# A mixture-of-experts layer on one core: all batches routed, results returned by accumulating DMA

## The chip, the cores and the metric

The kernel runs on one core of a Trainium2 chip. A core has five engines with a queue each: PE (TensorE, matrix products into PSUM), DVE (VectorE), ACT (ScalarE), POOL (GpSimd) and SP (SyncE, which here only starts DMA transfers). Each queue runs in order, and engines wait for one another by semaphores. Sixteen DMA engines move data between the chip's memory (HBM) and the on-chip memory (SBUF). The metric is the time of one execution in microseconds (us).

## The reference, cut to what matters

Sixteen sequences of 512 tokens with 256 numbers each go through a causal attention layer and a feed-forward layer, both behind a layernorm and with a residual:

```python
x = x + attention(layernorm(x))            # 16 heads of 64, soft-clamped scores
t = layernorm(x).reshape(-1, 256)          # 8192 tokens
shared = gelu(t @ sw1 + sb1) @ sw2 + sb2   # every token
probs = softmax(t @ gate_w + gate_b)       # 8 experts
topk_p, topk_i = top_k(probs, 2)           # two experts of each token
h = gelu(einsum('td,edf->etf', t, w1) + b1)
y = einsum('etf,efd->etd', h, w2) + b2
x = x + shared + sum over the two chosen experts of topk_p * y
```

All matrices of an expert are 256x256, and everything is float32.

## The kernel before, in words

**Attention.** The 16 batches run one after the other, and each as 8 pairs of heads. The loop at L826 steps over the 128 pairs. A step issues the scores of the next pair, attends the present one (`attend`), projects queries and keys of the pair after next (`project_qk`), and calls `around(b, p, fill)`, which places the rest of the work at fixed steps p of a batch. The order of PE is the program's own (L817); the other engines' queues are ordered by the compiler's scheduler, and the transfers of SP are held to the program's order (`sync_dma`).

**Feed-forward of the batch before.** Beside the attention of batch b, `around` does batch b - 1: its output projection (p = 0, 1), layernorm (p = 1), transposes, shared hidden layer and gate (p = 3), and at p = 4 `place` (where each token's two rows go), the shared output (`expert_out` with e = 8, where a product of `comb` and `b2_sb` at L722 adds all biases weighted by the gate) and `scatter` (eight indirect DMAs on POOL).

**Routing.** Batches 0 to 8 and 9 to 14 form two groups (L20). `scatter` writes each normalised token into two rows of `xs`, one region per expert. When a group is complete, `tabulate` works out which expert each tile of 256 rows belongs to (L84 gives the number of tiles: 43 and 31), and `routed_steps` puts one step per tile into a queue of fillers: load rows and weights two steps ahead (`fetch`, `fetch_weights`), hidden layer (`routed_hidden`), transposes of the next tile (`turned`), output of the tile before (`routed_out`), stored to `ys`. The queue is popped by `fill`, which spreads it over the remaining steps of attention.

**Gathers.** After the tiles come `pack` and `gather_steps`: for each 128 tokens two indirect DMAs fetch the rows of `ys` (L653), DVE scales and adds them to the residual, which had been kept in HBM (L668), and SP stores the result.

**Batch 15** is not routed. After the attention its feed-forward runs at L841 to L856, with the second group's fillers between: all eight experts on all 512 tokens (`hidden`, `expert_out`, L848 to L854), and the gathers of the second group beside them.

Of the kernel before, what the change touches and what calls it, by code (L numbers as in the profile page):

```python
# [19 lines left out]
GROUPS = (9, 6)  # L20
# [4 lines left out]
def preln_attention_moe_kernel(  # L25
# [23 lines left out]
    SH = E  # L49
    FC = w1.shape[3] // P  # L50
# [26 lines left out]
    class Group:  # L77


        def __init__(self, g, first, count):  # L80
            self.g, self.first, self.count = g, first, count
            self.tokens = count * N
            self.stride = self.tokens + SLOTS
            self.tiles = (2 * self.tokens + E * (SLOTS - 1)) // SLOTS  # L84
            self.rows = E * self.stride + E * SLOTS
            self.xs = dram.tile([self.rows, D], F32, tag=f"xs{g}", name=f"xs{g}")
            self.ys = dram.tile([self.tiles * SLOTS, D], F32, tag=f"ys{g}", name=f"ys{g}")
            self.kept = dram.tile([count, N, D], F32, tag=f"kept{g}", name=f"kept{g}")
            self.writes, self.stores = [], []
            self.slots, self.shares, self.places = {}, {}, None  # L90
            self.running = None
# [30 lines left out]
    b2_sb = weights("b2_sb", b2, nc.sync)  # L122
# [32 lines left out]
    zeros = const.tile([P, D], F32, tag="zeros", name="zeros")  # L155
    nc.gpsimd.memset(zeros, 0.0)

    def counting(name, n, step):
        i = const.tile([P, n], I32, tag=f"{name}_i", name=f"{name}_i")
        nc.gpsimd.iota(i, pattern=[[step, n]], base=0, channel_multiplier=0)  # L160
# [6 lines left out]
    by_slot = counting("by_slot", n_most, SLOTS)  # L167
    region = {}
    for group in dict.fromkeys(group_of.values()):
        region[group] = counting(f"region{group.g}", E, group.stride)  # L170
        for i in range(E):
# [4 lines left out]
                    zeros.unsqueeze(1).to_broadcast([P, SLOTS // P, D]),  # L176
                ).ins
            )
        group.places = const.tile(
            [P, group.count, NT, 2], F32, tag=f"places{group.g}", name=f"places{group.g}"  # L180
        )
# [4 lines left out]
    def layernorm(src, name):  # L186
# [10 lines left out]
        xn = work.tile([P, NT, D], F32, tag="xn", name=f"xn_{name}")  # L197
        for t in range(NT):
            nc.vector.tensor_scalar(  # L199
                xn[:, t, :],  # L200
# [161 lines left out]
    def gate(b, xT):  # L362

        pg = ps_m.tile([P, NT, E], F32, tag="m", name=f"pg_{b}")
        for t in range(NT):
# [29 lines left out]
        comb = small.tile([P, NT, 32], F32, tag="comb", name=f"comb_{b}")  # L395
        nc.gpsimd.memset(comb, 0.0)
        nc.gpsimd.memset(comb[:, :, E : E + 1], 1.0)
        nc.vector.scalar_tensor_tensor(
            comb[:, :, :E], rank, 1.5, pr, ALU.is_lt, ALU.mult
        )  # L400
        return comb, rank, pr

    def place(b, rank, pr):

        group = group_of[b]
        chosen = small.tile([P, NT, E], F32, tag="chosen", name=f"chosen_{b}")
# [10 lines left out]
        nc.vector.tensor_add(slot, pos, region[group].unsqueeze(1).to_broadcast([P, NT, E]))  # L417
        slots = const.tile([P, NT, 2], I32, tag=f"slots{b}", name=f"slots_{b}")
        shares = const.tile([P, NT, 2], F32, tag=f"shares{b}", name=f"shares_{b}")
        for i in range(2):  # L420
            own = small.tile([P, NT, 2, E], F32, tag="own", name=f"own_{b}_{i}")
            nc.vector.scalar_tensor_tensor(
                own[:, :, 0, :], rank, float(i), slot, ALU.is_equal, ALU.mult
            )
            nc.vector.scalar_tensor_tensor(
                own[:, :, 1, :], rank, float(i), pr, ALU.is_equal, ALU.mult
            )
            both = small.tile([P, NT, 2], F32, tag="both", name=f"both_{b}_{i}")
            nc.vector.tensor_reduce(both, own, AX.X, ALU.add)
            nc.vector.tensor_copy(group.places[:, b - group.first, :, i], both[:, :, 0])  # L430
            nc.vector.tensor_copy(shares[:, :, i], both[:, :, 1])
        nc.vector.tensor_copy(slots, group.places[:, b - group.first])
        group.slots[b], group.shares[b] = slots, shares
# [22 lines left out]
    def tabulate(group):  # L456
# [34 lines left out]
        which = small.tile([P, K], F32, tag="which", name=f"which_{g}", bufs=1)  # L491
# [23 lines left out]
        group.skip = skip  # L515
        for e in range(E):
            with queued():
# [3 lines left out]
                    zeros.unsqueeze(1).to_broadcast([P, SLOTS // P, D]),  # L521
            )
            unordered(f"xs{g}", inst, group.writes)

    def pack(group):

        g = group.g
        places = group.places.rearrange("p b t i -> p (b t i)")
        n_places = group.count * NT * 2
        over = small.tile([P, n_places, E - 1], F32, tag="table", name=f"over_{g}", bufs=2)  # L530
        nc.vector.tensor_tensor(
            over,
            places.unsqueeze(2).to_broadcast([P, n_places, E - 1]),
            region[group][:, 1:].unsqueeze(1).to_broadcast([P, n_places, E - 1]),
            ALU.is_ge,
        )
        nc.vector.tensor_mul(
            over, over, group.skip[:, : E - 1].unsqueeze(1).to_broadcast([P, n_places, E - 1])
        )
        back = small.tile([P, n_places], F32, tag="back", name=f"back_{g}", bufs=1)  # L540
        nc.vector.tensor_reduce(back, over, AX.X, ALU.add)
        nc.vector.tensor_sub(back, places, back)
        packed = const.tile([P, group.count, NT, 2], I32, tag=f"packed{g}", name=f"packed_{g}")
# [199 lines left out]
    def fill(p):  # L743

        if not fillers:
            return
# [162 lines left out]
```

## Time and profile before

| | |
|---|---|
| median of 3 runs | 2317.4 us (2316.65 to 2320.81) |
| the profiled execution | 2317.56 us, of which the span of its instructions is 2315.8 us |
| granted clock of PE | 0.993 of full speed |
| busy | PE 95%, DVE 48%, ACT 45%, POOL 41% of the span |
| batches 0 to 8 routed, first group's table | at 1151 us |
| second group's table | at 2061 us |
| last attention step's matmuls end | about 2096 us |
| output projection of batch 15 starts | 2104.4 us |
| dense experts of batch 15 start | 2238.4 us |
| moved by DMA | 161 MB |

The profile is of one execution. In its timelines a line gives start, duration, engine, line of the kernel, operation, and output<-input, and in square brackets how long the engine had stood idle and who released it. PE's instructions overlap, so the durations printed add up to more than the time; the difference between two starts is what an instruction costs. A float32 product counts as two instructions.

### The profile page before, as it was taken

To read this page: it belongs to the slowest core of one execution; us is meant where nothing else is said; L and a number is where in the kernel's file an instruction comes from. 1 tells how busy PE (TensorE), PEld (TensorE's weight loads), DVE (VectorE), ACT (ScalarE), POOL (GpSimd) and SP (SyncE) were. 2 spreads that over 40 slices of the span, in tenths; PEclk is the share of its full clock that TensorE was granted. 3 is DMA by queue.
4 is the path that set the end of the run, shared out by engine and by line. 5 is a ranking of instruction groups with operands and counts; after the bars stand their busy time and mean duration, and the time that the engine had idled before them with its cause. 6 is when DMAs were issued, how large, how long until landed. Compare 5 with 4: busy or idle time off the path is not lost.

```text
span 2315.8 us, 29554 instructions
## 1 busy us (share of the span) xinstructions
PE 2209.4 (95%) x10968; PEld 1405.6 (61%) x10968; DVE 1102.8 (48%) x1858; ACT 1037.9 (45%) x1352; POOL 952.3 (41%) x1091
## 2 busy tenths in 40 slices
PE   7999999999999999999999999999999799899996
PEld 3555555556565555555667677667655465558874
DVE  3445454545363636363644434444446555453334
ACT  3544444444444545444444554554554444351211
POOL 3444443435353535344423412422455847450025
PEclk9999999999999999999999999999999999999999
DMA  5001010101010101010142342342230503035776
GB/s 191 1 1 37 1 37 1 37 1 37 1 37 1 37 1 37 1 37 1 37 147 59 118 128 64 101 128 82 84 97 20 153 7 119 21 100 168 224 228 208
DMA packets 119855, 161.34 MB, mean 70 GB/s; under 512 B 12320, under 2 KB 90144, under 8 KB 119200
## 3 DMA queue, kind: packets, MB, share of 16 engines
q1 hardware_dynamic: 107760, 125.62, 17.5%
q0 software_dynamic: 11520, 31.47, 4.4%
q10 hardware_dynamic: 432, 2.36, 0.3%
q8 instruction: 87, 1.43, 0.3%
q14 instruction: 56, 0.46, 0.1%
HBM read 99.64 MB, written 59.77 MB: 69 GB/s over the span
## 4 chain that ended last, share of the span: by engine, by line
PE 76%; DVE 11%; DMA 5%; issue 3%; ACT 3%; POOL 2%; SPq 0%; POOLq 0%; DVEq 0%; ACTq 0%
PE pq L249 15%; PE s L272 10%; PE av L323 10%; PE po L353 9%; PE pv L232 8%; PE ry L604 5%; PE rh L586 5%; DVE oT L342 4%; PE sums L332 4%; DMA part<-ys,packed 3%; PE ph L695 2%; PE py L714 2%; DVE xn_a L199 2%; PE pr L573 1%; PE py L722 1%
## 5 line engine op out<-in xcount | busy, mean ns | idle before, releaser
L287 ACT ACTIVATE pe<-s 128x768 f32<-128x768 f32 (+1 forms) x384 | 334.5, 874 | 704.8 <-PE s L272 679.1
L342 DVE RECIPROCAL oT<-sums 128x256 f32<-128x256 f32 x256 | 430.9, 1724 | 355.3 <-PE sums L332 355.2
L291 POOL TENSOR_SCALAR_AFFINE_SELECT pe<-pe 128x256 f32<-128x256 f32 (+1 forms) x384 | 192.0, 501 | 902.0 <-ACT pe L288 847.4
L272 PE MATMUL s<-qk 64*128 64x512 f32 (+3 forms) x2048 | 345.4, 456 | 11.9 <-ACT qk L256 11.5
L288 ACT ACTIVATE pe<-pe 128x768 f32<-128x768 f32 (+1 forms) x384 | 349.5, 914 | 10.9
L323 PE MATMUL av<-pe,v 128*64 128x512 f32 (+3 forms) x2048 | 307.8, 443 | 34.5 <-DVE oT L343 34.4
L272 PEld LDWEIGHTS s<-qk 64*128 64x128 f32 x2048 | 176.6, 186 | 200.7 <-issue 144.9
L323 PEld LDWEIGHTS av<-pe,v 128*64 128x64 f32 x2048 | 140.3, 138 | 241.7 <-issue 208.7
L249 PE MATMUL pq<-xT_a,wq_sb 128*128 128x512 f32 x512 | 252.8, 617 | 0.8 <-DVE xT_a L217 0.8
L249 PE MATMUL pq<-xT_a,wk_sb 128*128 128x512 f32 x512 | 241.6, 595 | 5.0 <-DVE x L360 3.5
L232 PE MATMUL pv<-wv_sb,xT_a 128*128 128x256 f32 x1024 | 233.6, 382 | 4.4 <-DVE xT_a L217 4.4
L303 POOL TENSOR_TENSOR added<-pe,pe 128x768 f32<-128x768 f32 x128 | 232.3, 1814 | 10.5
L256 ACT COPY qk<-pq 128x512 f32<-128x512 f32 x256 | 149.8, 585 | 178.0 <-PE pq L249 178.0
L232 PEld LDWEIGHTS pv<-wv_sb,xT_a 128*128 128x128 f32 x1024 | 195.1, 192 | 52.0 <-issue 24.4
L353 PE MATMUL po<-wo_sb,oT 128*128 128x256 f32 x1024 | 226.3, 380 | 0.0
L353 PEld LDWEIGHTS po<-wo_sb,oT 128*128 128x128 f32 x1024 | 195.2, 191 | 38.7 <-issue 14.3
L653 POOL DMA_INDIRECT part<-ys,packed x120 | 117.2, 977 | 154.4 <-DMA dw<-in_w 99.6
L249 PEld LDWEIGHTS pq<-xT_a,wk_sb 128*128 128x128 f32 x512 | 97.7, 191 | 129.1 <-issue 120.4
L595 ACT ACTIVATE rhT<-rh,biases 128x256 f32<-128x256 f32 x148 | 62.0, 470 | 253.5 <-PE rh L586 253.4
L307 POOL TENSOR_TENSOR added<-added,pe 128x512 f32<-128x512 f32 x128 | 163.5, 1277 | 10.7
L239 DVE COPY v<-pv 128x512 f32<-128x512 f32 x128 | 87.3, 689 | 144.9 <-PE pv L232 144.9
L586 PE MATMUL rh<-rT,ew 128*128 128x256 f32 x592 | 142.6, 385 | 6.3 <-DVE rT L577 5.5
(134 smaller groups left out, 2302.4 us busy)
## 6 DMA issues: line engine op xcount, KB each, us to landing
ew<-in_w SPq DMA_DIRECT2D x148, 256.0 KB, 3.1
rows<-xs SPq DMA_DIRECT2D x74, 256.0 KB, 3.1
ys<-y SPq DMA_DIRECT2D x74, 256.0 KB, 3.3
x<-in_x SPq DMA_DIRECT2D x16, 512.0 KB, 4.0
xs<-zeros SPq DMA_DIRECT2D x32, 256.0 KB, 4.3
kept<-x SPq DMA_DIRECT2D x15, 512.0 KB, 3.0
acc<-kept SPq DMA_DIRECT2D x60, 128.0 KB, 2.9
out<-acc SPq DMA_DIRECT2D x60, 128.0 KB, 2.4
```

The lines of the kernel that those rows point to most:

```text
L232: nc.tensor.matmul(pv[:, u], xT[:, k, t * P : (t + 1) * P], wv_pairs[:, k, :, 2 * g : 2 * g + 2, :], start=(k == 0), stop=(k == KD - 1),)
L249: nc.tensor.matmul(pq, w[:, k, p * P : (p + 1) * P], xT[:, k, :], start=(k == 0), stop=(k == KD - 1),)
L272: nc.tensor.matmul(ps[:, i, at : at + w], qk[rows, 1, j * P : (j + 1) * P], qk[rows, 0, j * P :], start=True, stop=True,)
L287: nc.scalar.activation(pe[:, :, :w], ps[:, :, :w], AF.Tanh, scale=CLAMP_IN)
L288: nc.scalar.activation(pe[:, :, :w], pe[:, :, :w], AF.Exp, scale=SOFTCLAMP)
L291: nc.gpsimd.affine_select(out=diagonal, in_=diagonal, compare_op=ALU.is_ge, fill=0.0, base=0, pattern=[[0, 2], [0, n], [1, P]], channel_mu ...
L303: nc.gpsimd.tensor_tensor(added, pair_pe[b, p, 0][:, :, P:], pe[:, :, : N - P], ALU.add)
L307: nc.gpsimd.tensor_tensor(added[:, :, P:], added[:, :, P:], pe[:, :, : 2 * P], ALU.add)
L323: nc.tensor.matmul(po[i * DH : (i + 1) * DH, j * P :], v[:, j, i, p % 2, :], pair_pe[b, p, u][:, i, at : at + w], start=(j == 0), stop=(j ...
L342: nc.vector.reciprocal(oT[:, half], sums[:, half])
L353: nc.tensor.matmul(po[:, u, :], oTs[b, c][:, t * P : (t + 1) * P], wo_sb[:, c, :], start=(c == 0), stop=(c == NP - 1),)
L586: nc.tensor.matmul(ph[:, f, :], tile["w1"][:, d, f * P : (f + 1) * P], tile["T"][:, d, :], start=(d == 0), stop=(d == KD - 1),)
```

## The change

All 16 batches are routed, in groups of 12 and 4 (55 and 23 tiles by the same formula), so batch 15's dense pass goes. `xs` rows grow from 256 to 272 numbers: the tail holds the token's number and, for each of its two choices, slot, expert and gate value, which `place` writes behind the normalised token. The residual with the shared output is stored straight to `out` by SP. Each tile's result gets its expert's output bias by DVE (a fourth load per tile, spread over the partitions), is scaled on ACT by the token's share, and is added to the rows of `out` by two indirect DMAs of 128 rows each that accumulate in memory. Rows that hold no token carry a number past the bound and are left out. The pair of DMAs of a tile waits for the pair of the tile before, and the first pair of a group for the stores of its batches. `pack`, `gather_steps`, `comb` with its transpose, and the bias product on PE are gone; the shared output bias is added to the residual by POOL. Loads run three steps ahead. Sixteen steps of the first group are kept for the end.

The diff, cut to its core:

```diff
-GROUPS = (9, 6)
+GROUPS = (12, 4)
+META = 16
...
-            self.xs = dram.tile([self.rows, D], F32, tag=f"xs{g}", name=f"xs{g}")
-            self.ys = dram.tile([self.tiles * SLOTS, D], F32, tag=f"ys{g}", name=f"ys{g}")
-            self.kept = dram.tile([count, N, D], F32, tag=f"kept{g}", name=f"kept{g}")
+            self.xs = dram.tile([self.rows, ROW], F32, tag=f"xs{g}", name=f"xs{g}")
...
-    b2_sb = weights("b2_sb", b2, nc.sync)
+    sb2 = const.tile([P, D], F32, tag="sb2", name="sb2")
+    nc.sync.dma_start(sb2, b2[SH : SH + 1, 0].to_broadcast([P, D]))
...
     def place(b, rank, pr, xn2):
+        nc.gpsimd.memset(xn2[:, :, D:], 0.0)
...
+        nc.vector.tensor_scalar(xn2[:, :, TOK], by_token, float((b - B) * N), None, ALU.add)
         for i in range(2):
+            own = small.tile([P, NT, 3, E], F32, tag="own", name=f"own_{b}_{i}")
+            for j, of in enumerate((slot, expert, pr)):
+                nc.vector.scalar_tensor_tensor(
+                    own[:, :, j, :], rank, float(i), of, ALU.is_equal, ALU.mult
+                )
+            at = CHOICE + 3 * i
+            nc.vector.tensor_reduce(xn2[:, :, at : at + 3], own, AX.X, ALU.add)
+            nc.vector.tensor_copy(slots[:, :, i], xn2[:, :, at])
...
     def fetch_weights(group, tile):
+        tile["b2"] = work.tile([P, D], F32, tag="eb2", name=f"eb2_{g}_{k}", bufs=4)
+        sync_dma(tile["b2"], b2[bass.ds(e, 1), 0].to_broadcast([P, D]))
...
     def routed_out(group, tile):
-        y = work.tile([P, SUB, D], F32, tag="y", name=f"y_{g}_{k}", bufs=2)
-        nc.vector.tensor_copy(y, py)
-        inst = sync_dma(
-            group.ys[k * SLOTS : (k + 1) * SLOTS].rearrange("(u p) d -> p u d", p=P), y
+        y = work.tile([P, SUB, D], F32, tag="y", name=f"y_{g}_{k}", bufs=3)
+        nc.vector.tensor_add(y, py, tile["b2"].unsqueeze(1).to_broadcast([P, SUB, D]))
+        choices = tile["rows"][:, :, CHOICE : CHOICE + 6].rearrange("p u (i c) -> p u i c", c=3)
+        part = small.tile([P, SUB, 2], F32, tag="part", name=f"part_{g}_{k}", bufs=3)
+        nc.vector.scalar_tensor_tensor(
+            part, choices[:, :, :, 1], group.which[:, k : k + 1], choices[:, :, :, 2],
+            ALU.is_equal, ALU.mult,
         )
-        group.stores.append(inst)
+        share = small.tile([P, SUB], F32, tag="share", name=f"share_{g}_{k}", bufs=3)
+        nc.vector.tensor_reduce(share, part, AX.X, ALU.add)
+        tile["token"] = small.tile([P, SUB], I32, tag="token", name=f"token_{g}_{k}", bufs=3)
+        nc.vector.tensor_scalar(tile["token"], tile["rows"][:, :, TOK], float(B * N), None, ALU.add)
+        for u in range(SUB):
+            nc.scalar.activation(y[:, u], y[:, u], AF.Copy, scale=share[:, u : u + 1])
+        tile["y"] = y
+
+    def returned(group, tile):
+        insts = []
+        for u in range(SUB):
+            inst = nc.gpsimd.indirect_dma_start(
+                out=out.rearrange("b n d -> (b n) d"),
+                out_offset=bass.IndirectOffsetOnAxis(ap=tile["token"][:, u : u + 1], axis=0),
+                in_=tile["y"][:, u],
+                in_offset=None,
+                bounds_check=B * N - 1,
+                oob_is_err=False,
+                compute_op=ALU.add,
+            ).ins
+            to_results(inst, group.added or group.stores)
+            insts.append(inst)
+        group.added = insts
+
+    def to_results(inst, made):
+        tc.add_to_no_dep_group("results", inst)
+        behind(inst, made)
+        tc.declare_no_dep(inst, group="results", keep=made, reason="other tokens, or behind those kept")
...
         def step(k):
+            begin(k + 3)
             if k < 0:
-                begin(k + 2)
                 return
-            begin(k + 2)
...
-            if k >= 1:
-                routed_out(group, live.pop(k - 1))
+            if 1 <= k <= group.tiles:
+                routed_out(group, live[k - 1])
+            if k >= 2:
+                returned(group, live.pop(k - 2))
+        return [lambda k=k: step(k) for k in range(-3, group.tiles + 2)]
...
+    AT_END = 16
     def fill(p):
-        if not fillers:
+        if len(fillers) <= AT_END:
             return
-        pace["due"] += len(fillers) * WEIGHT[p] / max(pace["left"], WEIGHT[p])
+        pace["due"] += (len(fillers) - AT_END) * WEIGHT[p] / max(pace["left"], WEIGHT[p])
...
-            xns[done, 1] = layernorm(x_tiles[done], f"f{done}")
+            xns[done, 1] = layernorm(x_tiles[done], f"f{done}", ROW)
+            nc.gpsimd.tensor_tensor(
+                x_tiles[done],
+                x_tiles[done],
+                sb2.unsqueeze(1).to_broadcast([P, NT, D]),
+                ALU.add,
+            )
...
-            expert_out(done, SH, hTs.pop(done), sw2_sb, *gated[done])
+            shared_out(done, hTs.pop(done))
+            scatter(done, xns.pop((done, 1)))
+            inst = sync_dma(out[done].rearrange("(t p) d -> p t d", p=P), x_tiles.pop(done))
+            to_results(inst, [])
+            group.stores.append(inst)
+            if done == group.first + group.count - 1:
+                tabulate(group)
+                fillers.extend(routed_steps(group))
+                pace["left"], pace["due"] = (B - 1 - b) * sum(WEIGHT) + sum(WEIGHT[5:]), 0.0
...
-        for p, n in enumerate((4, 8, 0, 8, 4)):
+        for p, n in enumerate((1, 5, 0, 4, 0)):
             if p == 3:
                 early(B, p)
-                run(4)
+                run(1)
             around(B, p, lambda p: run(n))
-        comb, x2T = gated[b][0], xTs[b, 1]
-        ws = {e: dense_load(b, e) for e in range(2)}
-        hs = {0: hidden(b, 0, x2T, ws[0][0])}
-        for e in range(E):
...
-            expert_out(b, e, hs.pop(e), ws.pop(e)[1], comb, None)
-            run(-(-len(fillers) // (E - e)))
-        sync_dma(out[b].rearrange("(t p) d -> p t d", p=P), x_tiles.pop(b))
+        run(len(fillers))
```

## The prediction

> **What bounds the kernel now.** I read the page's busy shares and slices first, then TensorE's (PE's) order of time.
>
> ```profile
> PE 2209.4 (95%) x10968; PEld 1405.6 (61%) x10968; DVE 1102.8 (48%) x1858; ACT 1037.9 (45%) x1352; POOL 952.3 (41%) x1091
> ...
> PE   7999999999999999999999999999999799899996
> ```
>
> PE is busy nearly everywhere; the others are at half. So PE's work and PE's gaps are the time, except in the last slices. One instruction per batch, the transpose of L685, serves as a clock (timeline of PE; first column is the start):
>
> ```profile
> 1025.29 0.33 PE L685 MATMUL pc<-ident,comb 128*128 128x128 f32 x1 [0.28 <-DVE slot L417]
> 1142.83 0.33 PE L685 MATMUL pc<-ident,comb 128*128 128x128 f32 x1 [0.28 <-DVE slot L417]
> ...
> 1477.19 0.33 PE L685 MATMUL pc<-ident,comb 128*128 128x128 f32 x1 [0.28 <-DVE slot L417]
> 1647.39 0.33 PE L685 MATMUL pc<-ident,comb 128*128 128x128 f32 x1 [0.48 <-DVE slot L417]
> ...
> 1920.30 0.33 PE L685 MATMUL pc<-ident,comb 128*128 128x128 f32 x1 [0.28 <-DVE slot L417]
> 2051.96 0.33 PE L685 MATMUL pc<-ident,comb 128*128 128x128 f32 x1 [0.28 <-DVE slot L417]
> ```
>
> A plain batch takes 117.54 us, one filled with routed tiles 170.2, one filled with gathers 131.7. The gather batches hold no tile, so 14 us of each is stall. The list of waits of PE, 1700 to 1900 us (total, times, longest), says whose:
>
> ```profile
> PE av L323 <- DVE oT L343: 12.2, 5, 8.0
> PE pq L249 <- DVE x L360: 3.5, 1, 3.5
> PE sums L332 <- POOL added L308: 3.3, 3, 1.6
> ```
>
> VectorE (DVE) is late because its queue is in order and L668 waits there for gathered rows (39.3 us from 1700 to 2052 in DVE's own waits). What a routed tile costs PE is read between two hidden layers in the tail:
>
> ```profile
> 2143.56 1.89 PE L586 MATMUL rh<-rT,ew 128*128 128x256 f32 x8
> 2145.28 0.60 PE L573 MATMUL pr<-ident,rows 128*128 128x128 f32 x4
> 2145.72 1.89 PE L604 MATMUL ry<-ew,rhT 128*128 128x256 f32 x8
> 2147.45 1.89 PE L586 MATMUL rh<-rT,ew 128*128 128x256 f32 x8
> ```
>
> It is 3.89 us a tile, 0.216 us per 256-wide matmul; the printed durations overlap, so starts are what to subtract.
>
> **The change, up to the end of attention.** I add against this execution's span, 2315.8 us (2317.56 with what lies around it, 0.2 above the median of 2317.4).
>
> *Biases and L685.* One row tile's two matmuls of L722 move the next weight load by 0.43 us (2056.23 to 2056.66): 1.72 a batch. L685 with its wait is 0.4. A plain batch becomes 117.54 - 2.1 = 115.4. What replaces them is off PE: GpSimd (POOL) adds 128x1024 once a batch, 2.4 us by L303's 1.81 for 768; POOL is idle 59% of the time, and its next selections feed an attend a slot later. If that cover were gone, 16 x 2.4 = 38 us. DVE adds the second bias in the instruction that copied (L724's add costs 0.69, like L612's copy), plus three small operations of about 0.2; ScalarE (ACT) scales twice at about 0.47 (L595): 0.6 and 0.9 us per tile beside 3.89 of PE.
>
> *Gathers.* The six batches from 1142.83 to 2051.96 take 909.1; less 6 x 117.54 and 43 x 3.89 of tiles leaves 36.6 us for gathers, packing and tables. I take all of it off: DVE no longer waits for rows there. Bounds: 0 and 36.6.
>
> *Tiles.* Line 84 gives 55 and 23 tiles instead of 43 and 31. The 60 steps of the first group start three batches later; 44 run inside attention, 16 wait for the end. By the last L685 some 33.7 tiles are done instead of 43: 9.3 x 3.89 = 36.2 us earlier. So that point moves from 2052 to 2052 - 15 x 2.1 - 36.6 - 36.2 = 1947.6. From there to the last batch's output projection PE took 52.4 us, with 4.7 tiles (18.2), L722 and L685 (1.8) and 3.3 of stalls: 29.1 remain, and 7 tiles are added (27.2): it starts at 2004.
>
> **The tail.** The eight dense experts go (2238 to 2310, with the gathers beside them). PE still has projections, hidden, gate and shared, 24 us, 14.3 tiles of the first group and 23 of the second: 24 + 37.3 x 3.89 = 169. PE alone would end at 2004 + 169 = 2173; a wait for the last scatter's rows (5) and the last tile's way out (9: evacuation and scaling 2, the rest a pair and the end) make 2187.
>
> But each tile now ends in two accumulating DMAs on POOL, and a pair waits until the pair before has landed. The trace has no accumulate; its nearest rows, indirect DMAs of the same 128 rows of 1 KB (last figure: us from issue to landing):
>
> ```profile
> xs<-xn_f,slots POOLq DMA_INDIRECT x120, 2.4
> part<-ys,packed POOLq DMA_INDIRECT x120, 3.3
> ```
>
> and, from POOL's timeline and the chain that ended last:
>
> ```profile
> 2238.43 0.97 POOL L653 DMA_INDIRECT part<-ys,packed  x1 [0.30 <-issue]
> 2239.70 0.96 POOL L653 DMA_INDIRECT part<-ys,packed  x1 [0.31 <-issue]
> ...
> 2276.54 5.66 DMA part<-ys,packed
> ```
>
> A second DMA starts 1.27 us after the first, and a pair takes P = 1.27 + landing. From below: a scatter, 2.4, P = 3.7, faster than PE. From above: the slowest gather and then a scatter, 5.66 + 2.4, P = 9.3. An accumulate reads HBM as a gather does, beside weight loads as in this tail, where the chain's eight gathers average 4.56. I take that: P = 5.8.
>
> POOL's queue after 2004: layernorm's power operation and the bias add stand ahead of 10 of the 11 pairs that run before the scatter. They follow both halves of the projection and a tile (17.7), the layernorm (4.4 from L360 to L199 in this tail) and the add (2.4): POOL is free at 24.5 us. Then 9P and an issue (2.5), the last batch's clearing and slots (2.7: L417 to L432 took 1.7, plus a memset and two operations more), eight scatters at 1.27 (10). Behind these stand 5 + 23 = 28 more pairs: POOL ends at 2004 + 40 + 37P, plus 1.5. With three result buffers DVE, and behind it PE, can be three tiles ahead at most. P = 5.8 gives 2260 us; each us of P is worth 37. Added to the span as now: 2262.
>
> SyncE's queue drops a store per tile and gains a 128 KB bias load; it was 3.3 of 3.89 us busy per tile, now about 3.4: hidden unless the DMA engines are full (their share is 0.80 from 2140 to 2185). Rows grow from 1024 to 1088 bytes, and the sixteenth batch's placing costs PE some 1 us: both inside the rounding. At the start PE waits 14.3 us for the first batch, which the other bias load doesn't touch.
>
> Row and rule: gathers landed in 3.3 and 4.56 us. The Trainium skill, DMA: Bandwidth & Descriptors, Anatomy of one DMA — SWDGE (gpsimd) path, puts a transfer at about 2.0 us plus its bytes over 436 GB/s, an estimate of 2.3 for 128 KB; by that P is 3.6 and the end 2187. Against the change speaks Collectives: The Full Stack, The bandwidth ceiling: an add in the DMA path needs two source reads and runs at half a copy's rate. The trace's indirect DMAs fill the 16 engines for 0.42 us each (4.4% of the span over 240); twice that for a pair would add 0.8 to P, an estimate of 2291.
>
> **The rivals.**
>
> *PE bounds the tail* (P up to 4.6): 2187 to 2215. For it: the scatter's 2.4, and POOL stands empty in this tail from 2137 to 2237. Against: every gather in a loaded stretch took 3.5 or more. 0.17.
>
> *Slower: the accumulate is a gather and a scatter in sequence, generated at one and a half times the price.* Quiet rows 3.3 + 2.4, issue 1.75 for the pair's offset and 0.5 of queueing: P = 7.95, and 2004 + 41.5 + 37 x 7.95 = 2340, 2342 with what lies around. It decides from P = 7.3, where the sum meets 2316. Against: both rows hold the same fixed part (a POOL instruction is 0.96 of each), counted twice here. 0.17.
>
> *The gain in attention doesn't come*: POOL waits for an accumulate ahead of the selections of the next pair, or DVE for a result buffer. Before, POOL's lateness cost PE at most 1.6 us at a time; 44 pairs inside attention, 0 to 70 us. With the gathers' 36.6 kept, 2298; with 70, 2332. Against: pairs come one or two per slot of 15 to 23 us. 0.06 (0.04 slower).
>
> **How the numbers follow.** My forecast (P from 4.6 to 7.2) has 0.60. What a measurement can't tell from no change is 0.2%, here P within 0.12 of 7.3: 0.04, of which 0.03 are the forecast's edge and 0.01 the slower rival's. Faster: 0.17 + 0.57 + 0.02 = 0.76; slower 0.16 + 0.04 = 0.20; the same 0.04. The range runs from PE's bound, 2187, to P = 7.7, 2332; below it I leave 0.04, above 0.12.
>
> **What would show it.** The clock instruction is gone, but batches without fillers should be 115.4 apart, and filled ones without waits of `av` on `oT` beyond some 1 us. In the tail, starts of POOL's indirect pairs lie P apart and PE waits on DVE, DVE on a landing; a pitch of 3.9 with PE full means the first rival. If the last projection starts later than 2010, attention is the step that failed; if it starts there and the pitch isn't 5.8, the landing is. If PE's tiles wait for rows, loads and not the chain are late.

## The result and the profile after

The changed kernel takes **2487.3 us** (median of 4 runs, 2486.17 to 2488.76) against 2318.1 for the kernel before: a ratio of **1.073** (95% interval 1.071 to 1.075). The forecast was 2262. The profiled execution has a span of 2486.6 us, 226.6 more than the 2260 that the forecast set against it.

Busy shares and slices of the changed kernel:

```profile
PE 2225.3 (89%) x10716; PEld 1394.1 (56%) x10716; DVE 1089.4 (44%) x1925; ACT 1096.2 (44%) x1498; POOL 1117.0 (45%) x1136
...
PE   7999999999999999999999997988897897877665
PEclk9999999999999999999999998999998898988888
```

PE's busy time went up by 16 us although it has less work (10716 instructions, not 10968), and thirteen of its last sixteen slices are below 9. No other engine is above 45%: nothing is full, things wait. The eight lower clock digits all stand in slices with such holes.

L685 is gone as a clock; the second matmul of `pos` (L411) and the projection (L354) serve instead. PE's timeline, first column the start:

```profile
1039.61 0.39 PE L411 MATMUL pos<-ahead,ones 128*128 128x32 f32 x2
1159.38 0.39 PE L411 MATMUL pos<-ahead,ones 128*128 128x32 f32 x2
...
1518.30 0.39 PE L411 MATMUL pos<-ahead,ones 128*128 128x32 f32 x2
1697.36 0.39 PE L411 MATMUL pos<-ahead,ones 128*128 128x32 f32 x2
1891.51 0.39 PE L411 MATMUL pos<-ahead,ones 128*128 128x32 f32 x2
2093.49 0.39 PE L411 MATMUL pos<-ahead,ones 128*128 128x32 f32 x2
...
2167.85 7.07 PE L354 MATMUL po<-wo_sb,oT 128*128 128x256 f32 x32
```

A plain batch takes 119.6 us on average, not 115.4 (before: 117.5); filled ones take 179, 194 and 202. Cut at the same points as the forecast (1470.3 and 1947.6 are its own numbers: 1947.6 less three plain batches and 33.7 tiles), with two experiments that are told below:

| stretch, us | forecast | after | e3 | e9 |
|---|---|---|---|---|
| start to `pos` at the end of the plain batches | 1470.3 | 1518.3 | 1502.1 | 1480.8 |
| three filled batches | 477.3 | 575.2 | 499.1 | 498.5 |
| to the last projection | 56.4 | 74.4 | 56.0 | 56.2 |
| tail, from there to the end | 256 | 318.7 | 309.7 | 305.4 |

So 164 of the 227 us were lost inside attention and 63 in the tail. The forecast had named the sign for this: a last projection later than 2010 means that attention failed, and it starts at 2167.9. The list of DVE's waits in the changed kernel (total, times, longest) shows two that the kernel before did not have:

```profile
DVE token L595 <- DMA out<-y,token: 348.7, 67, 7.4
...
DVE xn_f L414 <- POOL xn_f L401: 99.8, 15, 7.2
```

L595 makes the integer row numbers that the two accumulating DMAs use. It reads nothing but a tile's loaded rows, so the scheduler places it in DVE's queue as early as its output buffer allows; there are three, and the fourth waits until an accumulate three tiles back has landed. In the first filled batch DVE's timeline, and the wait of PE that it ends in, look like this:

```profile
1664.91 0.17 DVE L595 TENSOR_SCALAR token<-rows 128x2 int32<-128x2 f32 x1 [6.40 <-DMA out<-y,token]
...
1671.24 0.48 DVE L595 TENSOR_SCALAR token<-rows 128x2 int32<-128x2 f32 x1 [5.93 <-DMA out<-y,token]
1671.63 0.67 DVE L588 SCALAR_TENSOR_TENSOR part<-rows,which 128x4 f32<-128x4 f32 x1
1672.22 3.36 DVE L343 RECIPROCAL oT<-sums 128x256 f32<-128x256 f32 x2
1675.50 0.62 DVE L218 COPY x2T_f<-pt_f 128x512 f32<-128x512 f32 x1
```

```profile
1676.27 4.61 PE L653 MATMUL ph<-x2T_f,sw_sb 128*128 128x512 f32 x5 [6.58 <-DVE x2T_f L218]
```

L414 writes the token's number into the tail of the layernorm tile; it follows POOL's clearing (L401), and that follows the last scatter, which still reads the one buffer of that name. DVE's timeline in a plain batch:

```profile
813.95 0.37 DVE L414 TENSOR_SCALAR xn_f<-by_token 128x4 f32<-128x4 f32 x1 [7.00 <-POOL xn_f L401]
814.22 0.68 DVE L679 TENSOR_TENSOR x<-x,py 128x512 f32<-128x512 f32 x1
814.82 3.36 DVE L343 RECIPROCAL oT<-sums 128x256 f32<-128x256 f32 x2
```

For 7 us DVE does nothing, and the reciprocals and the transposes' copies stand behind it. PE has other work for most of that time: in this stretch it stands idle only once, for 0.74 us before 818.87.

### The profile page after: what moved, and what is told of

Read it like the earlier page. It is cut to its first block, busy times and chain, and to the rows that moved or that the text cites. A ratio compares the mean times of both kernels' runs of the same rounds, so it can differ in the third digit from the quotient of the medians.

```text
span 2486.6 us, 29666 instructions
## 1 busy us (share of the span) xinstructions
PE 2225.3 (89%) x10716; PEld 1394.1 (56%) x10716; DVE 1089.4 (44%) x1925; ACT 1096.2 (44%) x1498; POOL 1117.0 (45%) x1136
## 5 line engine op out<-in xcount | busy, mean ns | idle before, releaser
L292 POOL TENSOR_SCALAR_AFFINE_SELECT pe<-pe 128x256 f32<-128x256 f32 (+1 forms) x384 | 198.9, 538 | 686.7 <-ACT pe L289 626.4
L604 POOL DMA_INDIRECT out<-y,token x156 | 242.3, 1553 | 409.2 <-ACT y L597 206.7
L324 PE MATMUL av<-pe,v 128*64 128x512 f32 (+3 forms) x2048 | 319.3, 455 | 30.7 <-DVE oT L344 30.7
L233 PE MATMUL pv<-wv_sb,xT_a 128*128 128x256 f32 x1024 | 244.1, 393 | 37.6 <-DVE xT_a L218 22.1
L559 PE MATMUL rh<-rT,ew 128*128 128x256 f32 x624 | 173.6, 427 | 90.8 <-DVE rT L550 78.3
L354 PE MATMUL po<-wo_sb,oT 128*128 128x256 f32 x1024 | 227.5, 380 | 0.0
L354 PEld LDWEIGHTS po<-wo_sb,oT 128*128 128x128 f32 x1024 | 195.6, 191 | 39.8 <-issue 12.9
L597 ACT ACTIVATE y<-y,share 128x256 f32<-128x256 f32 x156 | 70.9, 502 | 290.4 <-DVE y L585 261.2
L559 PEld LDWEIGHTS rh<-rT,ew 128*128 128x128 f32 x624 | 128.4, 211 | 124.5 <-DVE rT L550 90.8
L595 DVE TENSOR_SCALAR token<-rows 128x2 int32<-128x2 f32 x78 | 22.3, 286 | 348.8 <-DMA out<-y,token 348.7
```

Of the source, the lines that this page charges most:

```text
L233: nc.tensor.matmul(pv[:, u], xT[:, k, t * P : (t + 1) * P], wv_pairs[:, k, :, 2 * g : 2 * g + 2, :], start=(k == 0), stop=(k == KD - 1),)
L292: nc.gpsimd.affine_select(out=diagonal, in_=diagonal, compare_op=ALU.is_ge, fill=0.0, base=0, pattern=[[0, 2], [0, n], [1, P]], channel_mu ...
L324: nc.tensor.matmul(po[i * DH : (i + 1) * DH, j * P :], v[:, j, i, p % 2, :], pair_pe[b, p, u][:, i, at : at + w], start=(j == 0), stop=(j ...
L354: nc.tensor.matmul(po[:, u, :], oTs[b, c][:, t * P : (t + 1) * P], wo_sb[:, c, :], start=(c == 0), stop=(c == NP - 1),)
L559: nc.tensor.matmul(ph[:, f, :], tile["w1"][:, d, f * P : (f + 1) * P], tile["T"][:, d, :], start=(d == 0), stop=(d == KD - 1),)
L604: inst = nc.gpsimd.indirect_dma_start(out=out.rearrange("b n d -> (b n) d"), out_offset=bass.IndirectOffsetOnAxis(ap=tile["token"][:, u : ...
```

## The experiments

Four questions: what held DVE's queue, what an accumulate costs, what the biases are worth, and what remains. The kernel before ran beside each and took 2318 to 2321 us.

### DVE's queue: e1, e2, e3 and e15

e1 and e2 give the two tiles more buffers, e3 both.

```diff
-... name=f"token_{g}_{k}", bufs=3)                      # e1, e3
+... name=f"token_{g}_{k}", bufs=8)
-... tag=f"xn{width}", name=f"xn_{name}", bufs=1)        # e2, e3
+... tag=f"xn{width}", name=f"xn_{name}", bufs=1 if width == D else 2)
-... name=f"own_{b}_{i}")                                # e3, for room
+... name=f"own_{b}_{i}", bufs=1)
```

> The number tile of a routed tile gets eight buffers instead of three; nothing else. Theory B (buffers): operations that need only early data stand early in DVE's in-order queue and wait there for a buffer that an accumulating DMA has to free (L595 waited 349 us in all). Then filled batches fall from 194 to 202 us to some 170 to 180, the tail keeps its pitch of 8 us, and the whole takes 2400 to 2440 us. Theory C (chain): what costs is that a pair of DMAs waits on POOL for the pair before; the buffer is only where DVE notices it. Then nothing moves by more than 10 us from 2487.

> The layernorm tile that the scatter reads gets two buffers instead of one. In plain batches DVE stands 7 us at L414, behind a clearing on POOL (L401) that waits for the scatter of the batch before. Theory B: this goes; the step after it was 1.1 us longer than before the change, so a plain batch falls from 119.7 to about 118.6, a filled one by some 5, in all 2455 to 2475 us. What remains of the plain batch's excess over 115.4 (about 3 us) then has another cause, the bias addition on POOL that stands between two layernorms' power operations. Theory C: within 5 us of 2487.

> Eight number tiles and two layernorm tiles together (a helper tile of the placing goes from two buffers to one to make room). Theory B: the sum of the two, 2380 to 2425 us, with PE's waits on DVE in the filled batches mostly gone. Theory C: not under 2475. If both theories hold for one stage each, attention recovers here and the tail stays at 8 us a pair.

e1: 2409.3 us (1.040, 1.038 to 1.042). e2: 2448.4 (1.057, 1.055 to 1.059). e3: **2363.5** (1.019, 1.017 to 1.021), a little better than expected (2380 to 2425), and 123.8 us of the loss; the two edits alone gave 78.0 and 38.9. By the table most of it comes from the filled batches (76 us), 16 from the plain ones and 18 from the stretch before the projection; the tail moved by 9 only.

e15 leaves all buffers as the change has them and fixes only the place of these operations in DVE's queue:

```diff
+        held = tc.issue_after(nc.vector.tensor_add(y, py, ...).ins)     # L585
+        with held:
             part = scalar_tensor_tensor(...)                            # L588
+        with tc.issue_after(last["part"]):
             nc.vector.tensor_scalar(tile["token"], ...)                 # L595
```

> The changed kernel with its buffers as they are, and L588 and L595 held in VectorE's queue behind the addition of the same tile's result (L585), so that neither stands ahead of work that is due. If the order in VectorE's queue is what the eight token buffers of e1 mended, this alone gives at least as much: 2409 or less (2370 to 2415; the layernorm tile's single buffer is left as it is). If the number of buffers was the cause in itself (the accumulate holding a buffer that the next tile needs), the time stays above 2450.

2417.2 us (1.043, 1.040 to 1.045): 70 us back, nearly what five more buffers gave (78), though 2 us above the range expected. Inside attention the two are the same: the three filled batches take 513.7 us here and 513.0 in e1. The difference is in the tail, 323.9 against 307.1. So in attention it is the position of L595 in an in-order queue that costs. L414's place was not tried in this way, only its buffer (e2). More buffers end these two waits and not every wait: in e3 DVE waits 140.7 us in the tail for the three buffers of `y` (L585).

### The price of an accumulate: e4, e5, e6 and e8

Starts of the DMA pairs on POOL in the changed kernel, first in the loaded tail, then at its end, where no loads run any more:

```profile
2379.78 1.54 POOL L604 DMA_INDIRECT out<-y,token  x1 [5.10 <-DMA out<-y,token]
2381.63 1.54 POOL L604 DMA_INDIRECT out<-y,token  x1 [0.30 <-ACT y L597]
2387.98 1.54 POOL L604 DMA_INDIRECT out<-y,token  x1 [4.81 <-DMA out<-y,token]
...
2472.86 1.54 POOL L604 DMA_INDIRECT out<-y,token  x1 [1.95 <-DMA out<-y,token]
2474.71 1.54 POOL L604 DMA_INDIRECT out<-y,token  x1 [0.30 <-issue]
2478.23 1.54 POOL L604 DMA_INDIRECT out<-y,token  x1 [1.97 <-DMA out<-y,token]
```

The second DMA starts 1.85 us after the first, not 1.27: its instruction takes 1.54 us on POOL, where plain indirect ones take 0.97. A pair starts 8.2 us after the one before here, and 5.37 where nothing else runs. The wait in brackets is for the landing: the chain binds, as forecast, but with a longer P.

e6 is e3 with plain indirect writes in place of the accumulate, the chain kept; e8 is e3 without the tiles' weight loads.

```diff
-                compute_op=ALU.add,                                     # e6
...
-        sync_dma(tile["w1"], w1[:, bass.ds(e, 1)]...)                   # e8, and w2, b2
+        tile["w1"], tile["w2"], tile["b2"] = sw1_sb, sw2_sb, sb2
```

> Both buffer changes, chain kept, but the pairs write instead of accumulating (an output row keeps the last writer's part). This prices the accumulate. If it is dear by itself: the instruction falls from 1.54 to 0.97 us, the engines' share of a DMA from 0.82 to 0.42, and the pitch of the loaded tail from 7.9 to 5 or 5.5, in all 2260 to 2290. If the loads beside it make the landing long and not the adding, the pitch falls only by the instruction's 0.6 and the 0.8 of traffic, to about 6.8: 2315 to 2335.

> Both buffer changes, and every routed tile is computed with the shared expert's weights and bias, already on the chip, so a tile loads only its rows (272 KB instead of 912). If the loads beside it make the accumulate's landing long, the tail's pitch falls from 7.9 to near the 5.36 that the last two pairs show on quiet engines: 28 x 2 to 2.4, in all 2295 to 2310. If the pitch stays above 7, the long landing belongs to the accumulate in a running pipeline and not to the loads, and the time stays above 2345.

e6: 2311.5 us (0.996, 0.994 to 0.997), nearer to the second reading; e8: 2327.4 (1.004, 1.003 to 1.005), between the two. The times mix attention and tail; the pitch of the pairs is the cleaner answer. e6 in the loaded tail, and at the end:

```profile
2230.64 0.97 POOL L604 DMA_INDIRECT out<-y,token  x1 [4.03 <-DMA out<-y,token]
2231.92 0.98 POOL L604 DMA_INDIRECT out<-y,token  x1 [0.30 <-ACT y L597]
2236.61 0.97 POOL L604 DMA_INDIRECT out<-y,token  x1 [3.72 <-DMA out<-y,token]
...
2296.08 0.97 POOL L604 DMA_INDIRECT out<-y,token  x1 [1.90 <-DMA out<-y,token]
2297.35 0.98 POOL L604 DMA_INDIRECT out<-y,token  x1 [0.30 <-issue]
2300.26 0.97 POOL L604 DMA_INDIRECT out<-y,token  x1 [1.93 <-DMA out<-y,token]
```

| P, us (second issue + rest) | beside weight loads | without weight loads | nothing else |
|---|---|---|---|
| plain write (e6) | 1.28 + 4.9 = 6.2 | | 1.28 + 2.9 = 4.2 |
| accumulate (e3, e8, after) | 1.85 + 6.2 = 8.1 | 1.85 + 4.6 = 6.4 | 1.85 + 3.5 = 5.4 |

(Typical pairs of each stretch.) Adding costs 1.2 us a pair where nothing else runs and 1.9 beside loads, the weight loads some 1.7. Neither alone makes P: both theories are half right. The queue's share of the DMA engines, e3 and then e6 (packets, MB, share of 16 engines):

```profile
q0 software_dynamic: 28608, 34.65, 7.9%
```

```profile
q0 software_dynamic: 13632, 34.64, 4.1%
```

The same bytes take twice the packets. In e6, 4.1% of 2309.7 us over 284 indirect DMAs is 0.33 us each; with 128 of these taken off e3's 187 us, an accumulate fills the engines for 0.93, and 144 packets stand against 48.

The chain itself is what e4 and e5 take away: every pair adds into rows of its own, zeroed beforehand, and no pair waits for another. e4 does it on the changed kernel, e5 with e3's buffers.

```diff
+            self.ys = dram.tile([self.tiles * SLOTS, D], F32, ...)
-        nc.vector.tensor_scalar(tile["token"], tile["rows"][:, :, TOK], float(B * N), None, ALU.add)
+        nc.vector.tensor_scalar(tile["token"], by_token[:, :SUB], float(k * SLOTS), None, ALU.add)
-                out=out.rearrange("b n d -> (b n) d"),
+                out=group.ys,
-            to_results(inst, group.added or group.stores)
```

> As after, but each tile's pair accumulates into rows of its own in a zeroed scratch array (all 256 rows of a tile), so no pair waits for another; the routed results are left out of the output. Zeroing is 78 stores at the start beside other work. Theory C: attention's filled batches fall to about 165 us and the tail to PE's pace of 4 to 5 us a tile: 2300 us or less. Theory B: the tail falls to about 5 us a pair (28 x 3 = 85 us less), while the filled batches stay at 185 or more because DVE still waits for buffers: 2390 to 2420 us.

> Both buffer changes and no chain: each pair accumulates into zeroed rows of its own (all 256 rows), the routed results are left out of the output. If the buffers cost attention and the chain costs the tail, and nothing else does, the two gains add: 2363 less the tail's 28 pairs at about 5 instead of 7.9 us (81) is 2280, some 2270 to 2300. If the tail's pitch without a chain is set by the DMA engines (they hold 4.7 us of work per tile by their shares: 0.93 MB at 303 GB/s and two accumulates of 0.82), the pitch is 4.7 to 5 with PE waiting, and not PE's 3.9.

e4: 2387.0 us (1.031, 1.028 to 1.033), 3 us below the second theory's range there; its filled batches fell to 173, 181 and 185 and its tail by 71 us of the 85 expected. e5: 2358.4 (1.017, 1.015 to 1.018), far from the 2270 to 2300 expected. Its tail fell from 309.7 to 250.5 us, 59 of the 81 expected, with pairs some 5 us apart and the DMA engines 90% busy from 2180 to 2330, as expected. But attention lost 41 us to e3. DVE's waits of e5 from 1518 to 2098 say why:

```profile
DVE token L604 <- DMA ys<-y,token: 123.0, 36, 6.4
```

In this edit, as in e4, the row numbers depend on a constant only, not on loaded rows, so nothing holds the operation back and it ran ahead through all eight buffers. The experiment brought back the wait that it was meant to be free of. What the chain alone is worth is so read from the tail, 59 us, and not from the time.

### The biases: e7, e9 and e10

In e3 plain batches still take 117.9 us on average (118.6 and 117.0, mostly in turn). DVE's and POOL's timeline of e3 at the layernorm:

```profile
878.05 1.33 DVE L195 TENSOR_SCALAR ve_a<-mv_a 128x4 f32<-128x4 f32 x1
880.77 4.39 DVE L200 TENSOR_SCALAR xn_a<-x,mv_a,rstd_a 128x256 f32<-128x256 f32 x4 [1.38 <-POOL rstd_a L197]
```

```profile
877.01 2.35 POOL L720 TENSOR_TENSOR x<-x,sb 128x1024 f32<-128x1024 f32 x1 [1.39 <-DVE mv_a L193]
```

A 4-element operation of DVE that takes 0.17 us in e9 takes 1.33 here, and it ends (879.38) when POOL's addition ends (879.36). What PE then waits, first in e3 and then in e9, where the addition is left out:

```profile
889.30 2.37 PE L324 MATMUL av<-pe,v 128*64 128x512 f32 x16 [2.53 <-DVE oT L344]
```

```profile
876.56 2.37 PE L324 MATMUL av<-pe,v 128*64 128x512 f32 x16 [1.34 <-DVE oT L344]
```

e7 issues the addition later, behind POOL's next power operation:

```diff
-            nc.gpsimd.tensor_tensor(x_tiles[done], x_tiles[done], sb2..., ALU.add)   # p == 1
...
+                with tc.issue_after(last["rstd"]):                                   # p == 2
+                    nc.gpsimd.tensor_tensor(x_tiles[done], x_tiles[done], sb2..., ALU.add)
```

> Both buffer changes, and the bias addition on POOL is issued after the next batch's layernorm power operation instead of between the two. Theory: the addition holds DVE (its ve_a took 1.33 us beside it against 0.17) and puts the second power operation late, so PE waits 2.5 us for oT once a batch and runs at a lower clock after it. Then plain batches fall from 117.8 on average to 115.4 to 116 and the whole by 25 to 35 us, to about 2330. Rival: POOL is idle enough, and what remains in a plain batch is something else: less than 8 us.

2381.0 us (1.026, 1.024 to 1.028): slower than e3, against the expectation. `ve_a` is back at 0.17 us and POOL's power operation is on time, but now `xn_a` stands beside the addition. Its four passes, and the first of them alone:

```profile
882.31 5.40 DVE L200 TENSOR_SCALAR xn_a<-x,mv_a,rstd_a 128x256 f32<-128x256 f32 x4 [1.13 <-POOL rstd_a L197]
```

```profile
882.31 2.44 DVE L200 TENSOR_SCALAR xn_a<-x,mv_a,rstd_a 128x256 f32<-128x256 f32 x1 [1.13 <-POOL rstd_a L197]
```

That pass takes 0.49 us in e9. The microsecond has moved from one of DVE's operations to the next, and PE still waits 2.35 us for `oT`; so POOL's queue order is not what costs it. Why e7 is 18 us slower than e3 is open. The Trainium skill, SBUF — State Buffer, SBUF: two separate sides, says that DVE and POOL share one pair of ports which one of them locks for a whole instruction. It names as DVE's side operations that have two inputs there or run in a two-port mode. The end times agree with that (879.38 and 879.36 in e3, 884.75 and 884.60 in e7); no run here shows the ports themselves.

e9 leaves L720 out of e3 altogether.

> The changed kernel with both buffer fixes (2363.5 us), without the shared expert's output bias (GpSimd's L720 is left out, and with it that part of the result). If that GpSimd add is what keeps a plain batch at 117-118.6 us, wherever it is issued, plain batches fall to the predicted 115.4 to 116.2, the filled ones by 2 as well, and the time to 2335 (2325 to 2345). If something else does (the placing of the routed tokens, one-buffer tiles elsewhere), plain batches stay above 117 and the time between 2352 and 2365.

2342.8 us (1.010, 1.008 to 1.012): 20.6 us less than e3 (26.0 between the two profiled spans). 21.3 of the 26.0 come from the stretch of the plain batches (1502.1 to 1480.8), which are now 116.3 apart.

e10 asks the other side: what do L722 and L685 save in the kernel before, alone?

```diff
-        nc.vector.tensor_copy(y, py)
+        nc.vector.tensor_add(y, py, tile["b2"].unsqueeze(1).to_broadcast([P, SUB, D]))
...
             b, t, acc, parts = live.popleft()
+            nc.vector.tensor_add(acc, acc, sb2)
...
-                if e == SH:
+                if e == SH and b not in group_of:
                     nc.tensor.matmul(py[:, u, :], combT, ..., start=False, stop=True)
```

> The kernel before with one part of the change alone: no L685 and L722 for the 15 routed batches; an expert's bias is loaded per tile and added by VectorE in the instruction that copied, the shared one added by VectorE to each gathered row tile (60 additions), nothing on GpSimd. The step 'biases and L685' of the prediction gives 15 x 2.1 = 31 us: 2287 (2280 to 2294). If VectorE or ScalarE comes up as the next limit of a plain batch as soon as TensorE's two matmuls go, plain batches stay at 116.5 to 117.5 and the time at 2300 to 2318.

**2303.4 us, 0.993 of the kernel before (0.991 to 0.995): the fastest version that computes the whole result.** The gain is 0.7%. A plain batch takes 116.0 us: the edit is worth 1.5 us, not 2.1. The last projection starts 25 us earlier (2079.6 for 2104.6), of which the tail gave 10 back. PE waits 9.4 us for rows there, against 2.8 before; why is open.

### What remains in attention, and versions: e13, e11, e14 and e12

e9's three filled batches still take 498.5 us. Three plain ones and 34 tiles at 3.89 (the timeline shows 34; the expectation of e13 counts 32) make 481. With the buffers mended, DVE waits for something else, rows of tiles that are not due (e9, 1480 to 2035):

```profile
DVE part L588 <- DMA rows<-xs: 88.2, 35, 6.2
```

e13 is e9 with the hold of e15.

> e9 (both buffer fixes, the shared bias on GpSimd left out and with it that part of the result; 2342.8 us) with the same hold. If VectorE's 88 us of waiting for rows of later tiles is the 25 us that three filled batches still lose, they fall to 3 x 116.3 + 32 x 3.89 = 473 (470 to 485) and the time to 2322 (2315 to 2330). If the loss is GpSimd's (a pair of accumulating transfers with its wait ahead of the selections), filled batches stay at 495 or more and the time at 2338 to 2348.

2354.2 us (1.016, 1.014 to 1.018). The wait is gone from DVE's list, and the three batches take 496.2: 2 us less. So nearly all of these 88 us fell where PE had work. In the tail, where every result waits for its share, the hold costs 11 (316.4 for 305.4). The remaining 15 to 17 us go with PE waits of at most 4.8 us each; their cause is not settled.

e11 keeps less work for the tail: groups of 10, 4 and 2, eight steps for the end, and the shared bias in DVE's scaling of a tile. e14 is e11 with the hold.

```diff
-GROUPS = (12, 4)
+GROUPS = (10, 4, 2)
-    AT_END = 16
+    AT_END = 8
-            nc.scalar.activation(y[:, u], y[:, u], AF.Copy, scale=share[:, u : u + 1])
+            nc.vector.scalar_tensor_tensor(y[:, u], y[:, u], share[:, u : u + 1], sb2, ALU.mult, ALU.add)   # sb2 halved
```

> A version that could beat both: the changed kernel with both buffer fixes, groups of 10, 4 and 2 batches with 8 steps kept for the end in place of 16, and the shared bias added as two halves by VectorE in the instruction that scales a tile's rows (in ScalarE's place), nothing on GpSimd. By the measured 7.9 us a pair, 17 pairs fewer behind the last projection take 134 us off the tail (310 to 205 with the fixed part going down too), and 24 more tiles inside attention cost 93 us: 2330 (2310 to 2350). If the price of a pair inside attention is not hidden (GpSimd's queue holds the selections), filled batches stretch by more than 4 us a tile and the time is above 2360.

> e11 (groups of 10, 4 and 2, shared bias by VectorE, 2363.1 us) with the same hold. If a tile inside attention then costs 3.89 instead of 4.7, some 60 tiles give 45 us: 2318 (2305 to 2335), about the kernel before. If not, 2355 to 2368.

2363.1 us (1.019, 1.017 to 1.021) and 2363.3 (1.020, 1.018 to 1.022): both miss. The tail of e11 is 206.7 us, as expected. But by the trace 23 more tiles lie before the last projection (64 for 41; the expectation counts 24), and they took 110 us in place of 93 (it starts at 2145.3, against 2035.5 in e9). That is 4.8 us a tile, as the second reading there says, and the hold changed nothing. In these runs smaller groups only move the work.

e12 takes up the forecast's reading of the gathers: e10, with each gathered row tile finished two steps after it was asked for.

```diff
-            if i >= 1:
+            if i >= 2:
                 finish()
```

> The kernel before with its biases off TensorE (e10, 2303.4 us), and each gathered row tile finished two steps after it was asked for in place of one (four result buffers and six for gathered rows; the last batch's dense experts take turns on another buffer for room). The prediction put 36.6 us of the six filled batches down to VectorE waiting for gathered rows; in e10 the same stretch still holds 34.9 (898.3 less 6 x 116.02 less 43 x 3.89). If that reading is right, most of it goes: 2280 (2270 to 2290). If VectorE's waits for rows (32 us in e10) mostly fell into time in which TensorE had work, and the rest is packing and the tables, 2297 to 2305.

2315.1 us (0.999, 0.998 to 1.000): no gain, a loss of 12 against e10, and outside both readings. The edit did only part of what it was meant to do. In the three batches from 1631 us on, DVE's waits for gathered and for kept rows fell from 32.0 us (15.7 and 16.3) in e10 to 23.9 (19.8 and 4.1), and PE gained nothing by it. So e12 does not settle whether these waits are the stall of a gather batch. The longest wait of PE in such a batch of the kernel before shows two queues that are late together; DVE's and POOL's timelines, and PE's wait:

```profile
1840.90 1.19 DVE L668 SCALAR_TENSOR_TENSOR acc<-part,shares,acc 128x256 f32<-128x256 f32 x2 [0.55 <-DMA part<-ys,packed]
1842.01 3.36 DVE L342 RECIPROCAL oT<-sums 128x256 f32<-128x256 f32 x2
```

```profile
1831.05 0.97 POOL L653 DMA_INDIRECT part<-ys,packed  x1 [0.16 <-issue]
...
1839.89 0.95 POOL L653 DMA_INDIRECT part<-ys,packed  x1 [0.30 <-DMA part<-ys,packed]
1840.86 0.43 POOL L291 TENSOR_SCALAR_AFFINE_SELECT pe<-pe 128x256 f32<-128x256 f32 x1
...
1846.98 0.86 POOL L291 TENSOR_SCALAR_AFFINE_SELECT pe<-pe 128x512 f32<-128x512 f32 x1
```

```profile
1848.09 4.18 PE L323 MATMUL av<-pe,v 128*64 128x512 f32 x16 [7.98 <-DVE oT L343]
```

The wait ends with DVE's `oT` at 1847.94. The sums that it needs are there at 1831.8, but its reciprocals start only at 1842.01, behind additions that wait for gathered rows, as the forecast read it. At the same time eight gathers, about 1.26 us apart, stand in POOL's queue ahead of the three selections that this `av` reads; the last of these ends at 1847.84. So by this trace DVE's part alone would have bought little here. That is read and was not tried by itself.

## Why the prediction was wrong, step by step

- **Three small DVE operations per tile.** This is the step that failed. They were costed at 0.6 us beside PE's 3.89 by their duration alone, and the new operations of `place` on DVE at nothing in a plain batch, without a look at where L595 and L414 stand in DVE's queue and what their outputs wait for. Ending the two waits gave 123.8 us (e3). For L595 e15 shows that its place in the queue, not its work, is the cost in attention; for L414 (38.9 us alone, e2) only its buffer was tried. The third rival named DVE waiting for a result buffer, at 0 to 70 us and 0.06; it was the row-number buffer and the layernorm's, nearly twice that size, and in plain batches as well.
- **Shared bias on POOL, hidden.** The forecast gave nothing with the cover and 38 us without. It measured 20.6 (e9). That POOL was idle for much of the time was the wrong row to look at: the addition delays DVE.
- **L722 and L685, 2.1 us a batch.** It measured 1.5 (e10); why is open. In e9 a plain batch is 116.3, 0.9 above the forecast's 115.4.
- **Gathers, 36.6 us off.** That the gather batches hold stall was read rightly. That DVE's wait for rows is its cause stays open: e12 took away a quarter of that wait and gained nothing, and POOL's queue is late in the same place. In the change the pairs with their waits stand in POOL's queue too; whether that is why e9's filled batches keep 17 us over plain ones and tiles was not tried.
- **Tiles inside attention.** Right: 34 where 33.7 were counted, and once DVE's queue is mended the stretch to the last projection is 56.2 us (56.4 forecast).
- **The tail, 41.5 + 37P.** The chain binds, as forecast. P was mis-sized: 8.1 beside loads, not 5.8. By the same formula e9's 305.4 us mean a P of 7.1, since the pitch is not 8.1 throughout: pairs at the end run at 5.4. The forecast took the landing of a gather and the issue of a plain DMA; in e6 a plain write's pair takes 6.2, close to it. The accumulate adds the rest. The tail that is left in e9 is 49 us of the loss.
- **Row and rule.** The Trainium skill, Collectives: The Full Stack, The bandwidth ceiling, has the add of a collective's reduction at half a copy's rate; the forecast made that 0.8 us a pair. For a plain accumulating DMA the measurement says more: 0.93 us of the engines against 0.33, and 1.2 to 1.9 us a pair. The rule pointed the right way and was given no weight in the likeliest case.
- **The slower rival** (P = 7.95, issue 1.75 for the pair) came out almost as stated: issue 1.85, P 8.1. By itself it would have ended at 2342; e9, with the other causes out, is 2342.8. That agreement is luck: with e9's mean P of 7.1 the tail is 30 us shorter than in that sum, and attention is 31 longer.

In spans, the 226.6 us divide into 119.7 for DVE's queue (to e3), 26.0 for the bias on POOL (e3 to e9), and what e9 keeps over the forecast by stretch, 10.5 + 21.2 - 0.2 + 49.4 = 80.9. The last is a remainder by subtraction; of it the 49.4 of the tail have a cause above, and the 31.5 of attention do not.

## What to carry to other kernels

A cheap operation is not cheap if its inputs are ready early and its output buffer is freed late: in an in-order queue a scheduler puts it in front, and everything due stands behind it. So ask of each added operation what releases its output, and where it will stand. Giving its output more buffers and pinning it behind work that is due bought the same in attention (513.0 and 513.7 us for three filled batches); in the tail the pin was the slower by 17 us, and pinning on top of the buffers gained nothing in all (e13, e14). Price a chain of memory updates by its pitch under the load of that stage, since a pair took 5.4 us alone and 8.1 beside loads, and do not call an engine's operation hidden because that engine is idle.

## What the runs showed of the hardware

- An accumulating indirect DMA of 128 rows of 1 KB holds POOL for 1.54 us (0.97 without the add), fills the DMA engines for about 0.93 us (0.33) and makes 144 packets (48).
- An addition on POOL, two inputs of 128x1024, stretched a 4-element operation of DVE from 0.17 to 1.33 us, and one pass of `xn_a` from 0.49 to 2.44. The attention's own work on POOL does the same to `xn_a`, in the kernel before too, where its four passes take 4.38 us. In e9, a pass of `xn_f` with POOL idle, then a pass of `xn_a` and what POOL does beside it:

```profile
864.54 0.40 DVE L200 TENSOR_SCALAR xn_f<-x,mv_f,rstd_f 128x256 f32<-128x256 f32 x1
...
868.45 1.97 DVE L200 TENSOR_SCALAR xn_a<-x,mv_a,rstd_a 128x256 f32<-128x256 f32 x1
```

```profile
868.46 1.81 POOL L304 TENSOR_TENSOR added<-pe,pe 128x768 f32<-128x768 f32 x1
```

Again DVE ends 0.15 us after POOL. Four passes of `xn_f` take 1.6 us. Not every operation is held: in e3 the statistics of the layernorm (L192) take 0.43 and 0.41 us beside the same addition, as without it.
- A stall of PE can cost more than its length, and its length alone does not say when. In the tail of the changed kernel the next eight matmuls sometimes take up to twice as long, and sometimes not, after waits of about the same length:

```profile
2306.96 3.78 PE L559 MATMUL rh<-rT,ew 128*128 128x256 f32 x8 [3.21 <-DVE rT L550]
...
2409.28 1.99 PE L559 MATMUL rh<-rT,ew 128*128 128x256 f32 x8 [3.04 <-DVE rT L550]
```

The granted clock of the changed kernel is 0.93 of full speed between 1518 and 2168 and 0.86 from there on. In e9 it is 0.99 in the same batches, where PE's long waits are gone, and 0.84 in the tail, where they stay.
